# Involution weights laid out by frame row, and only the rows that are not zero written to DRAM

## The chip, the cores and the metric

The kernel runs on one core of one Trainium2 chip. The metric is the device time of one execution in microseconds. TensorE is PE in the profile, VectorE DVE, ScalarE ACT, GpSimd POOL, SyncE SP.

## What is computed

The input x is (32, 256, 32, 32). Two layers, each added to its input. The first is a group norm (32 groups of 8 channels) and a 3x3 convolution of 256 to 256 channels with values rounded to 16-bit floats. The second is a group norm and an involution: every pixel makes its own 7x7 kernel for each of 16 groups of 16 channels.

```python
# layer 1, xn = _gn(x)
y = relu(bn(einsum('oc,bchw->bohw', w1, xn)))              # 64 channels
w = einsum('oc,bchw->bohw', w2, y) + b2                    # 16 groups x 49 taps per pixel
w = w.reshape(b, G, K * K, H, W)
out = einsum('bgkhw,bgckhw->bgchw', w, patches)            # each output pixel: its 49 neighbours
x = x + out
```

## The kernel before, in words

The work goes image by image (32), and in each image by stages: 16 stages an image, of which every second has work of each kind. `front(b)` (L288 to L404) is a generator, run some 56 stages ahead of its image: group norm, the convolution (L336, 72 matmuls of 128x128 in 16-bit floats), second group norm into `xn`, the 64 channels `py` (L384), and the transposes `pt` (L399), copied to `pixels` (L403). `tc.manual_schedule()` (L549) keeps the order as the loop at L551 writes it, so every engine runs its instructions in this order; the framework adds the semaphores.

Multiplying each pixel by its own weights on TensorE is done by going through DRAM. A *frame* is a part of the image: 8 image rows (TR) by 16 columns (JC), in two halves of 4 rows (XR); each half of 64 partitions holds 4 rows x 16 columns as the contraction. An input pixel of a half adds to 10 rows (WIN = 4 + 7 - 1) by 22 columns of output around it. So for each input pixel a band row is wanted that holds, for each of 7 columns and 10 window rows, 16 groups: the weight where the output pixel is in reach of it, and zero elsewhere. The steps:

- `weights(b, r0)` (L406): 16 matmuls (each two instructions in the profile) make the weights `pw` of 4 image rows from `y_sb` and `w2_sb` (L414), for 32 columns in each of four column tiles.
- `evict` (L427) adds the bias on VectorE and writes them to the ring `w_sb` (L438). `w_sb` has 24 slots a pixel column, one for each image row. In this kernel a slot is [8 pairs of groups, 10 window rows, 2 groups of the pair], 160 floats of which three window rows are always zero; they are zeroed once (L207).
- `scatter(b, k, part)` (L468): seven DMAs a frame row, one per column tap, on SP's queue (L479). Each writes 32 columns x 8 rows of 160 floats (640 B) into the DRAM tensor `wd` [32 rows, 38 columns, 1128]. A pixel's record `WPIX` there is 7 x 160 floats and a padding of 8 floats that stays zero.
- `load_bands(b, k)` (L481): 16 DMAs a frame row bring, for pixel column j of both sides, 8 rows x 1128 floats (4512 B) to the partitions j, j+16, ... of a band tile. Successive rows are read `ROW - V` apart, so that each row lies shifted by one window row in its band. 14 of 16 go on POOL's queue, two on SP's (L491). There are three band tiles.
- `sums(b, m)` (L503): for both halves of groups h and both groups v of a pair, for both frame halves g and four column tiles t, one fp32 matmul (L517; two instructions in the profile). The moving operand `of` is taken from the band: 19 pixel columns (160 floats apart) by 10 window rows, for one group; at the image's upper and lower edge one of the two halves has 7 rows. It adds into `acc` in PSUM.
- `add_windows` (L525) adds `acc` to x on VectorE (L533); `store` writes x out.

The main loop puts, in each stage: the front's steps, `sums` of one frame, `add_windows` of the frame before, `weights` 18 stages ahead, `scatter`, the load of a later image (L590), `load_bands` three band tiles ahead. Before the loop, SP's queue gets, in order: image 0, the parameters, three zero fills of `wd` from a zeroed band (L200: the paddings of all 1216 records, and the side columns' taps that no scatter writes), and then image 1 and the following (L108). The profile's names: `wd<-w_sb` is the scatter, `band<-wd` the band load; L621 and L628 are the program's frame.

The two lines about which the rest turns:

```python
of = of.rearrange("p (j a r v) -> p j a r v", a=A, r=WIN, v=V)   # L514
of[:, :, a, f - top : l - top, v]                                  # L520, rows V = 2 floats apart
```

Of the kernel before, what the change touches and what calls it, by code (L numbers as in the profile page):

```python
# [9 lines left out]
F32 = mybir.dt.float32  # L10
# [3 lines left out]
P = 128  # L14
B, C, H, W = 32, 256, 32, 32
# [5 lines left out]
K1, PAD1 = 7, 3  # L21
TAPS = K1 * K1
CR = 64
G = 16
# [12 lines left out]
XR = 4  # L37
RG = 2
KP = P // RG
TR = RG * XR  # L40
SIDES = 2
JC = W // SIDES
K = H // TR
M = K * SIDES
WIN = XR + K1 - 1
WINC = JC + K1 - 1
WINI = JC + PAD1
# [4 lines left out]
V = 2  # L52
A = G // V
WB = G * WIN
PAD = V * (TR - XR)
WPIX = K1 * WB + PAD
SW = K1 * G
S = H + 2 * PAD1
T = 4
TW = P // T  # L60
PAIR = 3 * GC
PAIRS = G // 2
ROW = S * WPIX
WR = 4
NBAND = 3
SHARE = 8
NPIX = 6
RING = 24
# [6 lines left out]
def tile_quant_conv_then_involution(  # L75
# [16 lines left out]
    nc = tc.nc  # L92
    PSUM = bass.MemoryType.PSUM

    const = ctx.enter_context(tc.tile_pool(name="const", bufs=1))
# [47 lines left out]
    y_sb = [const.tile([P, N // 2], F32, name=f"y_{i}") for i in range(2)]  # L143
    bands = [const.tile([P, SIDES, WINC * WB + PAD], F32, name=f"band_{i}") for i in range(NBAND)]
    for t in bands[CH:]:
# [3 lines left out]
        nc.gpsimd.memset(t, 0.0)  # L149


    w_sb = const.tile([P, 2, RING, A, WIN, V], F32, name="w_sb")
    wd = dram.tile([H, S, WPIX], F32, name="wd")
    acc = [ps_acc.tile([P, RG, NT], F32, name=f"acc_{d}") for d in range(SIDES)]

# [9 lines left out]
    b2_sb = const.tile([P, 2, 2, SW], F32, name="b2_sb")  # L165
    for dj in range(K1):
        t, e = divmod(dj, 2)
# [19 lines left out]
    nc.vector.tensor_sub(bn_shift, bn[:, 1:2], bn_shift)  # L187


    for col, cols, at, n in (  # L190
        (0, S, K1 * WB, PAD),
        (PAD1, PAD1, 0, PAD1 * WB),
        (W, PAD1, (K1 - PAD1) * WB, PAD1 * WB),
    ):
        to = bass.AP(
            tensor=wd.tensor,
            offset=wd.offset + col * WPIX + at,
            ap=[[ROW, H], [WPIX, cols], [1, n]],
        )
        nc.sync.dma_start(to, bands[NBAND - 1][:H, 0, :n].unsqueeze(1).to_broadcast([H, cols, n]))  # L200

    def quantize_weights():

# [202 lines left out]
    def weights(b, r0):  # L406

        pws = [ps_w.tile([P, 2, 2, SW], F32, tag=f"pw{i}", name=f"pw{i}") for i in range(2)]
        for r in range(2):
            for t in range(T):  # L410
                for i in range(2):
                    half = slice(i * CR, (i + 1) * CR)
                    dj = slice(2 * t, min(2 * t + 2, K1))
                    nc.tensor.matmul(  # L414
                        pws[i][t * TW : (t + 1) * TW, : dj.stop - dj.start, r],
                        y_sb[b % 2][half, (r0 // 2 + r) * W : (r0 // 2 + r + 1) * W],
                        w2_sb[half, dj],
                        start=True,
                        stop=True,
                    )  # L420
        for i in range(2):
            for e in range(2):
                p = P if e == 0 else (K1 // 2) * TW
                for r, rows, d0, d1, at in ring_pieces(b, r0 + 2 * i):
                    evict(pws[i][:p, e, r : r + rows], e, r, rows, d0, d1, at)

    def evict(of, e, r, rows, d0, d1, at):  # L427

        p = of.shape[0]
        to = w_sb[:p, e]  # L430
        to = bass.AP(
            tensor=to.tensor,
            offset=to.offset + at * WB + V * (K1 - 1 - d0),
            ap=[to.ap[0], [V * WIN, rows * A], [WB - V, d1 - d0], [1, V]],
        )
        of = of.rearrange("p r (a d v) -> p (r a) d v", a=A, v=V)
        bias = b2_sb[:p, e, r : r + rows].rearrange("p r (a d v) -> p (r a) d v", a=A, v=V)
        nc.vector.tensor_tensor(to, of[:, :, d0:d1], bias[:, :, d0:d1], ALU.add)  # L438

    def ring_pieces(b, r0):  # L440
# [27 lines left out]
    def scatter(b, k, part):  # L468

        at = (b * H + k * TR) % RING  # L470
        for dj in range(part, K1, 2):
            t, e = divmod(dj, 2)
            to = bass.AP(
                tensor=wd.tensor,
                offset=wd.offset + k * TR * ROW + dj * WPIX + (K1 - 1 - dj) * WB,
                ap=[[WPIX, TW], [ROW, TR], [1, WB]],
            )
            rows = w_sb[t * TW : (t + 1) * TW, e, at : at + TR]
            nc.sync.dma_start(to, rows.rearrange("p s a r v -> p s (a r v)"))  # L479

    def load_bands(b, k):  # L481

        band = bands[(b * K + k) % NBAND]
        for i in range(JC):
            j = i // 2 + i % 2 * JC // 2
            src = bass.AP(
                tensor=wd.tensor,
                offset=wd.offset + k * TR * ROW + (j + PAD1) * WPIX,
                ap=[[ROW - V, TR], [JC * WPIX, SIDES], [1, WPIX]],
            )  # L490
            queue = nc.sync if i % SHARE == SHARE - 1 else nc.gpsimd  # L491
            queue.dma_start(band[j::JC, :, j * WB : j * WB + WPIX], src)  # L492

    def windows(b, m):


        k, d = divmod(m, SIDES)
        for g in range(RG):
            top = k * TR + g * XR - PAD1
            at = acc[d][:, g, : CH * WINI * WIN].rearrange("p (h j r) -> p h j r", h=CH, r=WIN)  # L500
            yield g, at, top, max(top, 0), min(top + WIN, H)

    def sums(b, m):  # L503

        k, d = divmod(m, SIDES)
        j0 = 0 if d else PAD1
        band = bands[(b * K + k) % NBAND][:, d]
        px = pixels[(b * K + k) % NPIX][:, d]
        for h in range(CH):
            for v in range(2):  # L510
                for g, at, top, f, l in windows(b, m):
                    p = slice(g * KP, (g + 1) * KP)
                    of = band[p, V * g * XR + j0 * WB : V * g * XR + (j0 + WINI) * WB]
                    of = of.rearrange("p (j a r v) -> p j a r v", a=A, r=WIN, v=V)  # L514
                    for t in range(T):
                        a = h * T + t
                        nc.tensor.matmul(  # L517
                            at[t * TW : (t + 1) * TW, h, :, f - top : l - top],
                            px[p, a, v * GC : v * GC + TW],
                            of[:, :, a, f - top : l - top, v],  # L520
                            start=(h, v) == (0, 0),
                            stop=(h, v) == (CH - 1, 1),
                        )
# [25 lines left out]
    with tc.manual_schedule():  # L549
        fronts = {}  # L550
        for n in range(FRONT, B * per + 2):  # L551
# [14 lines left out]
            if b is not None and i % 2 == 0:  # L566
                sums(b, i // 2)
# [14 lines left out]
            for part in range(2):  # L582
                b, i = due(n, -LEAD + 1 + part)
                if b is not None and i % 2 == 0:
                    for k in range(K):
                        if i // 2 == min((k + 1) * TR // WR, H // WR - 1):
                            scatter(b, k, part)
# [5 lines left out]
            if b is not None and i % 4 == 0:  # L593
                load_bands(b, i // 4)
# [37 lines left out]
```

## Time and profile before

| | |
|---|---|
| median of 3 runs | 1384.38 us (1379.81 to 1394.09) |
| the profiled execution's own time | 1388.26 us |
| its span, first to last instruction | 1386.5 us |
| PE busy, share of the span | 1265.7 us, 91% |
| DVE, ACT, POOL | 62%, 52%, 73% |
| granted PE clock, mean | 0.982 |
| DMA packets, bytes | 366568, 369.97 MB, mean 267 GB/s |
| `wd<-w_sb` | 896 DMAs of 160.0 KB |
| `band<-wd` | 1792 on POOL, 256 on SP, of 70.5 KB |
| waits: PE acc L517 on DMA band<-wd | 45.8 us in 21 waits |

How to read it. The span is one profiled execution; the few us around it make the device time. A busy share is the time in which at least one instruction of the engine runs; matmuls overlap, and the share of a line or form counts the union of its own. In a group's line, "x" is the number of instructions, then busy us and mean ns of one, then the idle time of the engine just before them and who ended it. The slices are 40 equal parts of the span, each digit the busy tenths. DMA share is the mean busy share of 16 engines. The chain of waits is followed back from the last instruction; "SPq" is SyncE's time to issue a DMA.

### The profile page before, as it was taken

How to read it: one execution, taken by the hardware profiler on the slowest of the kernel's cores; microseconds unless marked ns; L12 is line 12 of the kernel's file. 1: busy time of each engine (PE TensorE's matmuls, PEld its weight loads, DVE VectorE, ACT ScalarE, POOL GpSimd, SP SyncE). 2: the span in 40 equal slices, each digit the busy share in tenths (PEclk: the TensorE clock that was granted, in tenths of full speed). 3: DMA queues.
4: the chain of work that ended last, by engine and by line, in shares of the span. 5: the costliest groups of instructions: out<-in, count | busy, mean ns of one | idle time of the engine just before them, and what ended most of it. 6: DMA issues, size and time to landing. Idle time of an engine off the chain costs nothing.

```text
span 1386.5 us, 70020 instructions
## 1 busy us (share of the span) xinstructions
PE 1265.7 (91%) x29440; PEld 809.6 (58%) x29440; DVE 861.2 (62%) x3179; ACT 727.1 (52%) x1699; POOL 1010.0 (73%) x1818
## 2 busy tenths in 40 slices
PE   4799999999999999999999999999999998999763
PEld 2356666666665655566566666656666665656542
DVE  3366666666666666676676666657666675766542
ACT  4765555465646545665455565645556564553300
POOL 9067677687777777777768687777787767778785
PEclk9999999999999999999999999999999999999987
DMA  6089999999999999999999999999999999999995
GB/s 220 2 223 283 282 272 289 281 267 297 277 268 282 285 281 274 278 282 272 289 280 282 284 276 276 286 287 268 280 303 272 283 286 276 276 275 271 269 268 170
DMA packets 366568, 369.97 MB, mean 267 GB/s; under 512 B 78960, under 2 KB 308528, under 8 KB 366000
## 3 DMA queue, kind: packets, MB, share of 16 engines
q1 hardware_dynamic: 280240, 235.90, 57.6%
q0 software_dynamic: 86016, 129.60, 33.8%
q8 instruction: 234, 3.83, 1.2%
q14 instruction: 78, 0.64, 0.2%
HBM read 184.43 MB, written 180.76 MB: 263 GB/s over the span
## 4 chain that ended last, share of the span: by engine, by line
PE 58%; DMA 24%; POOL 5%; issue 4%; DVE 3%; ACT 3%; SPq 2%; POOLq 0%; DVEq 0%; ACTq 0%
PE pc L336 22%; PE acc L517 19%; DMA band<-wd 13%; PE pw L414 11%; DMA wd<-w_sb 9%; POOL band L492 5%; PE py L384 3%; PE pt L399 3%; DVE w_sb L438 2%; ACT junk L223 1%; SPq L479 1%; DMA w_sb<-in_w 1%; DVE x L533 0%; ACT xn L282 0%; DMA x<-in_x 0%
## 5 line engine op out<-in xcount | busy, mean ns | idle before, releaser
L492 POOL DMA_DIRECT2D band<-wd x1792 | 978.0, 548 | 363.0 <-DMA band<-wd 218.5
L438 DVE TENSOR_TENSOR w_sb<-pw,b_sb 128x16 f32<-128x16 f32 (+9 forms) x1920 | 373.7, 265 | 423.9 <-PE pw L414 403.5
L336 PE MATMUL pc<-xq,wq 128*128 128x496 f16 (+3 forms) x2304 | 535.8, 379 | 27.4 <-ACT xq L282 23.8
L517 PE MATMUL acc<-band,pixels 64*32 64x190 f32 (+1 forms) x16384 | 427.1, 330 | 68.5 <-DMA band<-wd 45.8
L336 PEld LDWEIGHTS <-wq 128*128 128x128 f16 x2304 | 206.8, 98 | 322.6 <-issue 110.1
L517 PEld LDWEIGHTS acc<-band,pixels 64*32 64x32 f32 x16384 | 301.7, 106 | 157.9 <-issue 86.1
L414 PE MATMUL pw<-w_sb,y 64*32 64x224 f32 (+1 forms) x8192 | 292.9, 332 | 17.0 <-issue 15.2
L533 DVE TENSOR_TENSOR x<-acc,x 128x380 f32<-128x380 f32 (+1 forms) x512 | 262.7, 513 | 32.8 <-PE acc L517 23.9
L414 PEld LDWEIGHTS pw<-w_sb,y 64*32 64x32 f32 x8192 | 187.7, 106 | 48.3 <-issue 31.1
L403 ACT COPY pixels<-pt 128x512 f32<-128x512 f32 x128 | 73.7, 576 | 237.5 <-PE pt L399 237.5
L223 ACT ACTIVATE junk<-x 128x512 f16<-128x512 f32 (+1 forms) x192 | 146.4, 763 | 20.1 <-DVE x L352 8.4
L223 ACT ACTIVATE junk<-x,mean 128x1024 f16<-128x1024 f32 x128 | 147.1, 1149 | 4.3
L254 ACT ACTIVATE s<-back,eps 128x2 f32<-128x2 f32 x64 | 18.9, 296 | 204.8 <-DVE back L239 204.7
L350 DVE TENSOR_SCALAR q<-pc 128x512 f16<-128x512 f32 x128 | 87.2, 682 | 19.3 <-PE pc L336 19.2
L282 ACT ACTIVATE xn<-x,off,rstd 128x512 f32<-128x512 f32 x128 | 96.2, 800 | 0.0
L352 DVE SCALAR_TENSOR_TENSOR x<-q,bias_sb,x 128x512 f32<-128x512 f16 x128 | 94.7, 740 | 0.3
L399 PEld LDWEIGHTS pt<-ident,xn 128*128 128x128 f32 x512 | 63.7, 142 | 25.9 <-issue 3.2
L399 PE MATMUL pt<-ident,xn 128*128 128x128 f32 x512 | 77.8, 275 | 0.1
L282 ACT ACTIVATE xq<-x,off,rstd 128x1024 f16<-128x1024 f32 x64 | 75.7, 1227 | 0.5 <-PE pc L336 0.5
L384 PEld LDWEIGHTS py<-xn,w_sb 128*64 128x64 f32 x2048 | 62.7, 138 | 16.6 <-issue 7.5
L244 ACT ACTIVATE mean<-back 128x2 f32<-128x2 f32 x64 | 12.7, 198 | 111.5 <-DVE back L239 111.4
L384 PE MATMUL py<-xn,w_sb 128*64 128x64 f32 x2048 | 67.6, 224 | 2.6 <-ACT xn L282 1.9
(40 smaller groups left out, 370.8 us busy)
## 6 DMA issues: line engine op xcount, KB each, us to landing
wd<-w_sb SPq DMA_DIRECT2D x896, 160.0 KB
band<-wd POOLq DMA_DIRECT2D x1792, 70.5 KB, 4.9
x<-in_x SPq DMA_DIRECT2D x64, 512.0 KB
out<-x SPq DMA_DIRECT2D x64, 512.0 KB
band<-wd SPq DMA_DIRECT2D x256, 70.5 KB
band<-in_w SPq DMA_DIRECT2D x2, 1152.0 KB
w_sb<-in_w SPq DMA_DIRECT2D x2, 196.0 KB
wd<-band SPq DMA_DIRECT2D x2, 180.0 KB
```

The costliest lines, as they stand in the source:

```text
L223: nc.scalar.activation(junk[:, n0:n1], src[:, h, n0:n1], func, bias=bias, accum_out=self.sums[:, i : i + 1])
L282: nc.scalar.activation(dst, src, AF.Identity, bias=self.off[:, one], scale=self.rstd[:, one])
L336: nc.tensor.matmul(pc.rearrange("p (r c) -> p r c", c=W)[:, r0 - nt * RT : r1 - nt * RT, c0:c1], wq[:, kh, k, mh * P : (mh + 1) * P], xq[: ...
L350: nc.vector.tensor_scalar(q, pc, F16_MAX, -F16_MAX, ALU.min, ALU.max)
L352: nc.vector.scalar_tensor_tensor(xt[:, mh, cols], q, bias_sb[:, mh : mh + 1], xt[:, mh, cols], ALU.add, ALU.add)
L384: nc.tensor.matmul(py[i * CR : (i + 1) * CR, cols], w1_sb[:, kh, :], px[:, r : r + 2], start=kh == 0, stop=kh == CH - 1,)
L399: nc.tensor.transpose(pt[:, i, h * P : (h + 1) * P], xn[:, h, (m + i) * P : (m + i + 1) * P], ident)
L414: nc.tensor.matmul(pws[i][t * TW : (t + 1) * TW, : dj.stop - dj.start, r], y_sb[b % 2][half, (r0 // 2 + r) * W : (r0 // 2 + r + 1) * W], w ...
L438: nc.vector.tensor_tensor(to, of[:, :, d0:d1], bias[:, :, d0:d1], ALU.add)
L492: queue.dma_start(band[j::JC, :, j * WB : j * WB + WPIX], src)
L517: nc.tensor.matmul(at[t * TW : (t + 1) * TW, h, :, f - top : l - top], px[p, a, v * GC : v * GC + TW], of[:, :, a, f - top : l - top, v], ...
L533: nc.vector.tensor_tensor(x_at, of, x_at, ALU.add)
```

## The change

A slot of `w_sb` becomes [7 rows, 16 groups], 112 floats, with no zeros. The scatter writes 112 floats (448 B) where it wrote 160. In `wd` a pixel's record keeps ten window rows for each of seven taps, now as [10 rows, 16 groups]; the padding becomes 16 x 4 = 64 floats, so a record has 1184 floats (4736 B). The three zero rows of each tap are no longer written by the scatter: `wd` is zeroed whole, once, at the place of the three small fills, by one DMA of 5.76 MB (32 x 38 x 4736 B) from a zeroed band on 32 partitions. Bands are loaded in records of 4736 B with rows `ROW - 16` apart. The moving operand of `sums` takes group a * 2 + v of each row: rows 16 floats apart. The columns of w2 and b2 are put in the new order on the host. Instructions, their number and order stay as they are, except that SP issues one fill in place of three.

```diff
-PAD = V * (TR - XR)
+SLOT = G * K1
+PAD = G * (TR - XR)
 WPIX = K1 * WB + PAD
...
-    w_sb = const.tile([P, 2, RING, A, WIN, V], F32, name="w_sb")
+    w_sb = const.tile([P, 2, RING, SLOT], F32, name="w_sb")
...
-    for col, cols, at, n in (
-        (0, S, K1 * WB, PAD),
-        (PAD1, PAD1, 0, PAD1 * WB),
-        (W, PAD1, (K1 - PAD1) * WB, PAD1 * WB),
-    ):
-        to = bass.AP(
-            tensor=wd.tensor,
-            offset=wd.offset + col * WPIX + at,
-            ap=[[ROW, H], [WPIX, cols], [1, n]],
-        )
-        nc.sync.dma_start(to, bands[NBAND - 1][:H, 0, :n].unsqueeze(1).to_broadcast([H, cols, n]))
+    zeros = bands[NBAND - 1][:H, 0, :WPIX].unsqueeze(1).to_broadcast([H, S, WPIX])
+    nc.sync.dma_start(wd, zeros)
...
-            offset=to.offset + at * WB + V * (K1 - 1 - d0),
-            ap=[to.ap[0], [V * WIN, rows * A], [WB - V, d1 - d0], [1, V]],
+            offset=to.offset + at * SLOT + G * (K1 - 1 - d0),
+            ap=[to.ap[0], [SLOT, rows], [SLOT - G, d1 - d0], [1, G]],
         )
-        of = of.rearrange("p r (a d v) -> p (r a) d v", a=A, v=V)
-        bias = b2_sb[:p, e, r : r + rows].rearrange("p r (a d v) -> p (r a) d v", a=A, v=V)
+        of = of.rearrange("p r (d g) -> p r d g", g=G)
+        bias = b2_sb[:p, e, r : r + rows].rearrange("p r (d g) -> p r d g", g=G)
...
-                ap=[[WPIX, TW], [ROW, TR], [1, WB]],
+                ap=[[WPIX, TW], [ROW, TR], [1, SLOT]],
             )
             rows = w_sb[t * TW : (t + 1) * TW, e, at : at + TR]
-            nc.sync.dma_start(to, rows.rearrange("p s a r v -> p s (a r v)"))
+            nc.sync.dma_start(to, rows)
...
-                ap=[[ROW - V, TR], [JC * WPIX, SIDES], [1, WPIX]],
+                ap=[[ROW - G, TR], [JC * WPIX, SIDES], [1, WPIX]],
...
-                    of = band[p, V * g * XR + j0 * WB : V * g * XR + (j0 + WINI) * WB]
-                    of = of.rearrange("p (j a r v) -> p j a r v", a=A, r=WIN, v=V)
+                    of = band[p, G * g * XR + j0 * WB : G * g * XR + (j0 + WINI) * WB]
+                    of = of.rearrange("p (j r g) -> p j r g", r=WIN, g=G)
...
-                            of[:, :, a, f - top : l - top, v],
+                            of[:, :, f - top : l - top, a * V + v],
```

The zero fill stands at L191 and L192 of the changed kernel, the scatter at L471, the band load at L484 and the matmul of `sums` at L509.

More of the change, by code (lines that the diff above doesn't have):

```diff
@@ L605 @@
     v = {name: np.asarray(a) for name, a in inputs.items()}
-    w2 = v["L1_conv_w2"].reshape(A, V, K1, K1, CR).transpose(4, 3, 0, 2, 1).reshape(CR, K1, K1 * G)
-    b2 = v["L1_conv_b2"].reshape(A, V, K1, K1).transpose(3, 0, 2, 1).reshape(K1, K1 * G)
+    w2 = v["L1_conv_w2"].reshape(A, V, K1, K1, CR).transpose(4, 3, 2, 0, 1).reshape(CR, K1, K1 * G)
+    b2 = v["L1_conv_b2"].reshape(A, V, K1, K1).transpose(3, 2, 0, 1).reshape(K1, K1 * G)
     laid_out = {
```

## The prediction

> **What bounds the kernel now.** I read the page's slices first, then stretches of the middle, then the groups by form, the waits and the start.
>
> ```profile
> PE   4799999999999999999999999999999998999763
> DMA  6089999999999999999999999999999999999995
> ...
> q1 hardware_dynamic: 280240, 235.90, 57.6%
> q0 software_dynamic: 86016, 129.60, 33.8%
> ```
>
> Two resources are full from the third slice to the third from the end: TensorE and the 16 DMA engines. The stretches say how full.
>
> ```profile
> core 0: us, PE busy (x) PEld busy (x) DVE busy (x) ACT busy (x) POOL busy (x), PEclk, DMA share, GB/s
> 600.00:643.00 43.00, 40.81 (x992) 26.89 (x976) 28.78 (x115) 23.76 (x57) 30.02 (x56) 0.96 1.00 288
> 700.00:743.00 43.00, 41.61 (x999) 26.81 (x979) 28.55 (x108) 22.69 (x54) 32.19 (x59) 1.00 0.99 284
> 1300.00:1343.00 43.00, 27.39 (x872) 20.35 (x880) 22.21 (x92) 3.26 (x6) 33.98 (x64) 0.92 0.92 267
> ```
>
> In the middle PE is idle for 2.19 and 1.39 us of 43 (mean 1.8) and DMA for nothing: both are bounds. The first `sums` matmul of image 0 starts at 93.9 us, of image 29 at 1277.9 (starts of L517 in the trace): 29 images in 1184.0 us, 40.8 each, PE idle about 1.7 of each (1.8 x 40.8/43) or 49 us in all. After 1278 no convolution is left, and there DMA (0.92) is ahead of PE. So relieving DMA alone can win at most the 49 us and a little at the end, while a microsecond added to PE's work per image is paid 29 times, less that same idle time.
>
> ```profile
> 703.41 1.56 PE L517 MATMUL acc<-band,pixels 64*32 64x190 f32 x64
> 704.65 1.07 PE L414 MATMUL pw<-w_sb,y 64*32 64x224 f32 x32
> 705.66 2.08 PE L336 MATMUL pc<-xq,wq 128*128 128x496 f16 x9
> ```
>
> From the timeline (start, length): one stage on PE. A `sums` call holds PE from 703.41 to 704.65, 1.24 us: 64 instructions, eight at once (two row halves, four column tiles), so eight turns of 155 ns.
>
> ```profile
> L517 PE MATMUL acc<-band,pixels 64*32 64x190 f32 x12288 | 424.4, 337 | 52.4 <-DMA band<-wd 32.1 <-issue 9.9 <-DMA wd<-w_sb 5.5
> L414 PE MATMUL pw<-w_sb,y 64*32 64x224 f32 x6144 | 290.7, 355 | 12.4 <-issue 11.0 <-DVE w_sb L438 1.0
> L517 PE MATMUL acc<-band,pixels 64*32 64x133 f32 x4096 | 184.4, 309 | 16.2 <-DMA band<-wd 13.7 <-issue 2.5
> L414 PE MATMUL pw<-w_sb,y 64*32 64x112 f32 x2048 | 180.2, 265 | 4.6 <-issue 4.1
> ```
>
> The groups by form (mean ns after the comma) price a column. L414 reads w2_sb without gaps: 112 columns more cost 355 - 265 = 90 ns, 0.80 ns a column. L517 reads rows 8 B apart, 19 pixel columns of 10 or 7 rows. Its 57 columns more should cost 46 ns; they cost 337 - 309 = 28. If instead rows are served in pairs and an odd row costs a whole pair, seven rows count as eight: 19 x 2 = 38 places x 0.80 = 30 ns. That fits. So the trace says that a row which shares its 16 B with no neighbour costs about two places.
>
> ```profile
> 22.28 0.67 SPq L200
> ...
> 23.00 0.73 SPq L200
> ...
> 23.77 0.43 SPq L200
> ...
> 24.24 0.44 SPq L108
> ...
> 24.72 5.63 DMA x<-in_x
> ```
>
> The chain at the start: the zero fills of L200, then the load of image 1 behind them on the same queue, then ScalarE, which waited 2.92 us for that load (its timeline at 29.19). This place has no slack.
>
> **The change part by part.** The instructions of each engine keep their kind, number and order; only SP has two DMAs less. Durations are those of the profiled execution: 1388.26 us, span 1386.5, and 3.9 above the median of 1384.38 that the forecast is to be held against.
>
> *The moving operand of L517.* `of` takes one group of 16 for each row: rows stand 64 B apart instead of 8. No two rows of a pixel share 16 B. From the odd row above, each of the 190 rows then costs two places: 190 x 0.80 = 152 ns more per turn. The half with 133 columns is always beside one with 190, which sets the turn. Eight turns, 1.22 us a call; eight calls, 9.8 us an image; 29 images, +284 us. PE has no room for it. Bounds: below, nothing, if the pairing is not what the odd row showed (the vector add L533 reads PSUM rows 40 B apart and takes 543 ns for 380 elements, as much per element as L352's 740 for 512, so strides are not dear everywhere). Above: the starts of successive matmuls on one tile in the trace have a median distance of 170 ns for 190 columns and 147 for 133, where 57 x 0.80 would leave 124; 23 ns over 19 odd rows is 1.2 ns each, so 230 ns a turn, 14.7 us an image, +427 us. I take 152, by the nearest row, the form that differs in nothing else.
>
> [...]
>
> *Scatter, L479.* 896 DMAs of 256 packets (229,376, as the trace's packet records have them), 640 B each, now 448 B. A 640 B packet takes 32 ns in the median, 36.0 in the mean. 448 B packets are in the trace, the loads of b2_sb: 25 ns in the median. The smallest writes to DRAM there, 32 B, take 7; on the line from 7 to 32, 448 B gives 24. I take 0.75 of the time: 9.0 ns x 229,376 / 16 engines = 129 us of engine time less. Bounds: 0.70 (bytes alone), and 55 ns a packet, what the slowest twentieth of the 640 B packets take (rival 3).
>
> [...]
>
> *Band loads, L492.* 2048 DMAs of 16 packets, 4512 B, now 4736: mean 242 ns x 5% x 32,768 / 16 = +25 us. Net DMA -104 us, 3.2 an image of some 40. What that buys: PE's idle time in the middle, 49 us, which is largely waiting for bands and buffers; a longer PE image hides the rest too. I take three quarters, -37; bounds 0 and -49. It can't be had twice, so once PE is the longer by 9.8, faster transfers bring nothing more.
>
> *The zero fill, L190.* One DMA of 1216 packets of 4736 B in place of three small ones, on SP's queue ahead of images 1 to 3. The old fill has 192 packets of 1920 B from the same 32 partitions, 148 ns each: at that rate 365 ns x 1216 / 16 = 27.7 us, less the old fills' 2.3: +25 us. Lower bound by the 640 B packets' rate, 20 B/ns: 18 - 2 = +16; by the 4512 B packets' 181 ns: 14.4 - 2.3 = +12. I take 25 because packet sources and moment are the same. Behind it: image 1's load, ScalarE's stream (in order, so image 0's second half too), the second convolution at 40.4. SP's two issues less save 1 us. Nothing later gives it back, since both bounds run at their rate from 94 us on.
>
> *Evictions, L438.* Runs of 16 instead of 2. 224 elements take 383 ns and 16 take 164, 1.05 ns an element already with runs of 2; nothing to win, and VectorE is 62% busy. *Memsets on POOL:* w_sb is 30% smaller (6.5 us, now 4.5), each band 1.6% larger; they end by 33 us, the first reader of w_sb comes at 62.
>
> *The last three images.* 35 to 37 us each, with DMA ahead; PE has some 12 us of room in each against +9.8. DMA is 3 us shorter. I take +2 in all.
>
> Sum: +284 - 37 + 25 + 2 = +274; 1388.3 + 274 = 1662 on the profiled execution, 1658 on the median.
>
> **The rivals.**
> 1. *Stride costs PE nothing (the other side, faster).* The turn stays at 155 ns, DMA falls under PE: -37 in the middle, -9 at the end (3 an image), +25 at the start: -21, 1363 on the median. With the fill at +12, 1350; with no idle time won back, up to 1395. For it: DMA at 1.00 and the waits for band<-wd; against it: the 133-column form. Each ns on a turn costs 64 x 29 = 1.86 us, so it decides as long as a turn grows by less than 11 ns.
> 2. *The single rows cost more than two places,* by the distances of starts: +427 - 49 + 25 + 9 (PE passes DMA in the last images as well) = +412, 1796. For it: the medians; against: the means by form. Between 1 and the forecast lies half a penalty, +142 - 37 + 25 = +130, 1514, if the four tiles, whose groups now lie 8 B apart, are served in part together.
> 3. *Short writes become dear and DMA the bound* without PE's penalty: packets at 55 instead of 36.0 ns, 19 x 229,376 / 16 = +272, bands +25, fill +25: 1706. For it: nothing in the rows; against: 32 B at 7 ns. Together with PE's penalty PE and DMA are about equal again, near 1720.
>
> **How the numbers follow.** Two places for each row 0.58 (with rival 3 on top or not): 1658, own range 1620 to 1720. Rival 2: 0.12. Half a penalty: 0.11. Rival 3 alone: 0.04. Rival 1: 0.15, of which 0.12 is under the bound of 1% (about what a measurement of this kernel can tell from no change) and 0.03 within it. Faster 0.12, same 0.03, slower 0.85. The range from 1500 to 1800 leaves out rival 1 and the edges of the half penalty.
>
> **What would show it.** Right: L517's 64x190 form about 150 ns longer and the 64x133 form about 90 (266 places for 152); `sums` calls about 2.4 us apart from the next L414 instead of 1.24; DMA share in the middle near 0.75 and PE without gaps; images 49 to 50 us apart; image 1's load landing near 55 us and the first L517 near 119; scatter packets at 24 to 25 ns. Wrong: L517's form unchanged (rival 1), or packets of 448 B at 50 ns and DMA still at 1.00 (rival 3). My sum fails first at the price of a single row, which the trace shows only one in seven at a time, never in a run.

## The result, and the profile after

The changed kernel takes 1633.46 us in the median (1633.11 to 1637.68), the kernel before 1387.32 beside it: a ratio of 1.1795, 95% interval 1.1752 to 1.1838, slower. The profiled execution took 1637.68 us with a span of 1635.9; its span is 249.4 us longer than that of before, where the working had +274.

The slices of the page of the kernel after, its queues and its memory traffic:

```profile
PE   4399999999999999999999999999999999999995
...
DMA  7458788877787877788877778877878877877796
...
q1 hardware_dynamic: 280016, 198.13, 44.0%
q0 software_dynamic: 86016, 136.02, 33.2%
...
HBM read 191.77 MB, written 142.07 MB: 204 GB/s over the span
```

PE is full and DMA no longer is: two bounds have become one. The start has changed too: the second and third slice of PE show 3 and 9 where 7 and 9 stood, in slices that are 18% longer.

The stretches of the kernel after (width, busy of each engine, PE clock, DMA share, GB/s):

```profile
600.00:643.00 43.00, 43.00 (x808) 27.46 (x807) 24.95 (x91) 21.98 (x52) 25.90 (x49) 1.00 0.76 198
700.00:743.00 43.00, 43.00 (x820) 27.85 (x809) 23.16 (x84) 21.17 (x47) 29.30 (x54) 1.00 0.79 197
1300.00:1343.00 43.00, 43.00 (x822) 27.26 (x827) 24.19 (x99) 21.51 (x51) 25.72 (x49) 1.00 0.77 201
```

PE is busy 43.00 of 43 us at clock 1.00, and it gets through 808 to 822 matmuls where it did 992 and 999. Nothing is awaited; the matmuls themselves are longer. DMA is at 0.76 to 0.79 (it was 1.00).

The timeline of PE of the kernel after, one stage (start, length):

```profile
727.53 3.05 PE L509 MATMUL acc<-band,pixels 64*32 64x190 f32 x64
730.12 1.21 PE L406 MATMUL pw<-w_sb,y 64*32 64x224 f32 x32
731.27 2.08 PE L328 MATMUL pc<-xq,wq 128*128 128x512 f16 x9
```

The `sums` call holds PE from 727.53 to 730.12, 2.59 us where it held it for 1.24; the convolution behind it is as long as before (2.08 us). The weights between them take 1.21 us here and took 1.07, but their matmuls are no longer, as the groups show. The groups by form of the kernel after (count, busy us, mean ns):

```profile
L509 PE MATMUL acc<-band,pixels 64*32 64x190 f32 x12288 | 745.6, 505 | 8.5 <-DMA band<-wd 8.5
L406 PE MATMUL pw<-w_sb,y 64*32 64x224 f32 x6144 | 348.6, 354 | 0.0
L509 PE MATMUL acc<-band,pixels 64*32 64x133 f32 x4096 | 281.5, 415 | 4.2 <-DMA band<-wd 3.1 <-issue 1.1
L406 PE MATMUL pw<-w_sb,y 64*32 64x112 f32 x2048 | 220.3, 265 | 0.0
```

The two forms of `sums` are 168 ns (337 to 505) and 106 ns (309 to 415) longer, where the prediction named about 150 and 90; the two forms of the weights are not longer at all (355 and 265 before). So it isn't the clock (1.00 here) and isn't PE as such: only the matmul whose operand's rows moved apart.

The start, from the chain of waits of the kernel after (start, length):

```profile
22.45 0.67 SPq L192
23.16 31.41 DMA x<-in_x
```

and from its ScalarE timeline (in brackets the idle time before and its releaser):

```profile
54.67 1.06 ACT L215 ACTIVATE junk<-x 128x1024 f16<-128x1024 f32 x1 [27.71 <-DMA x<-in_x]
```

The load of image 1 stood 5.63 us in the chain; now it stands 31.41, because the zero fill is ahead of it on its queue. ScalarE, which waited 2.92 us for it, waits 27.71. The granted PE clock is not behind the later start: it was 0.50 for longer (39.2 to 69.9 us, before 38.7 to 45.5), but from the end of that load to the first `sums` matmul it took 64.2 us, and 63.5 before.

By the starts of the `sums` matmuls in the trace the whole difference can be laid out:

| | before | after |
|---|---|---|
| first `sums` matmul | 93.9 us | 118.8 us |
| mean distance of images 0 to 29 | 40.83 us | 48.71 us |
| PE idle in these 29 images | 51.4 us | 0.0 us |
| PE's own time of an image (distance less idle) | 39.05 us | 48.71 us |
| from image 29 to PE's last instruction | 103.4 us | 99.0 us |

### The profile page after: what moved, and what is told of

It is laid out like the page before. It is cut to its first block, busy times and chain, and to the rows that moved or that the text cites. A ratio compares the mean times of both kernels' runs of the same rounds, so it can differ in the third digit from the quotient of the medians.

```text
span 1635.9 us, 70020 instructions
## 1 busy us (share of the span) xinstructions
PE 1563.9 (96%) x29440; PEld 997.0 (61%) x29440; DVE 862.5 (53%) x3179; ACT 730.8 (45%) x1699; POOL 1006.5 (62%) x1818
## 3 DMA queue, kind: packets, MB, share of 16 engines
HBM read 191.77 MB, written 142.07 MB: 204 GB/s over the span
## 4 chain that ended last, share of the span: by engine, by line
PE 91%; DMA 4%; ACT 2%; SPq 1%; DVE 1%; issue 1%; POOL 0%; POOLq 0%; ACTq 0%; DVEq 0%
PE acc L509 41%; PE pc L328 29%; PE pw L406 14%; PE py L376 4%; PE pt L391 3%; DMA x<-in_x 2%; ACT junk L215 1%; DMA band<-wd 1%; DMA w_sb<-in_w 1%; POOL band L484 0%; DMA wd<-w_sb 0%; SPq L180 0%; ACT xn L274 0%; DVE w_sb L430 0%; SPq L170 0%
## 5 line engine op out<-in xcount | busy, mean ns | idle before, releaser
L484 POOL DMA_DIRECT2D band<-wd x1792 | 977.4, 548 | 614.4 <-DMA wd<-w_sb 214.6
L509 PE MATMUL acc<-band,pixels 64*32 64x190 f32 (+1 forms) x16384 | 747.3, 482 | 12.6 <-DMA band<-wd 11.5
L509 PEld LDWEIGHTS acc<-band,pixels 64*32 64x32 f32 x16384 | 434.5, 119 | 200.9 <-issue 71.3
L406 PE MATMUL pw<-w_sb,y 64*32 64x224 f32 (+1 forms) x8192 | 348.7, 332 | 0.0
L406 PEld LDWEIGHTS pw<-w_sb,y 64*32 64x32 f32 x8192 | 250.9, 112 | 43.7 <-issue 8.2
```

The source lines that it names most:

```text
L406: nc.tensor.matmul(pws[i][t * TW : (t + 1) * TW, : dj.stop - dj.start, r], y_sb[b % 2][half, (r0 // 2 + r) * W : (r0 // 2 + r + 1) * W], w ...
L509: nc.tensor.matmul(at[t * TW : (t + 1) * TW, h, :, f - top : l - top], px[p, a, v * GC : v * GC + TW], of[:, :, f - top : l - top, a * V + v],
```

## The experiments

Two theories stood to be told apart. The one on record: a row that is alone in its 16 B (below: in its *line*) costs PE two *places*, a place being the time of one column, some 0.8 ns. Its rivals: the loss is DMA's (short runs, longer records, the fill); the loss is PE's but from the size of the step, from wide fetches or from four tiles whose groups now lie side by side. Where an edit makes PE read other numbers of the band, the text on record says so. Ratios are against runs of the kernel before on the same chip.

**Only the read, in the kernel before.**

```diff
-                    of = of.rearrange("p (j a r v) -> p j a r v", a=A, r=WIN, v=V)
+                    of = of.rearrange("p (j w) -> p j w", w=WB)
...
-                            of[:, :, a, f - top : l - top, v],
+                            of[:, :, a * V + v + 16 * (f - top) : a * V + v + 16 * (l - top - 1) + 1 : 16],
```

> The kernel before, with one edit: the moving operand of sums takes its rows 64 B apart from the same bands (it multiplies other numbers of the band; scatter, fills and bands are those of before). Theory (a row alone in its 16 B costs two places): the turn goes from 168 to about 320 ns, images come 48.7 us apart with PE never idle, so 93.9 + 29 x 48.7 + about 102 = 1608 us of span, ratio 1.16. Rival (the loss comes from the DMA side, the new runs, records and fill): the turn stays at 168 and the time at that of before, ratio 1.00.

Measured: 1607.56 us, ratio 1.1619 (1.1561 to 1.1677). Its groups by form and a stretch of the middle:

```profile
L517 PE MATMUL acc<-band,pixels 64*32 64x190 f32 x12288 | 743.4, 504 | 12.3 <-DMA band<-wd 10.9 <-DVE x L533 1.3
...
L517 PE MATMUL acc<-band,pixels 64*32 64x133 f32 x4096 | 282.2, 414 | 4.1 <-DMA band<-wd 4.1
```

```profile
600.00:643.00 43.00, 43.00 (x827) 26.17 (x814) 22.08 (x69) 19.97 (x48) 27.15 (x51) 1.00 0.84 236
```

504 and 414 ns, the numbers of the changed kernel (505 and 415), with scatter, fills and records as they were. Images come 48.65 us apart. One edit of the read is the whole loss per image; DMA's rival is out.

**All of the change but the read.**

```diff
-                    of = of.rearrange("p (j r g) -> p j r g", r=WIN, g=G)
+                    of = of.rearrange("p (j a r v) -> p j a r v", a=A, r=WIN, v=V)
...
-                            of[:, :, f - top : l - top, a * V + v],
+                            of[:, :, a, f - top : l - top, v],
```

> The changed kernel, with one edit: the moving operand takes its rows 8 B apart again (it multiplies other numbers of the band). Theory: the turn is back at 168 ns; the shorter scatter leaves DMA below PE, images come at PE's own 39.1 to 39.6 us, the fill still costs 25 us at the start: 118.8 + 29 x 39.4 + 99 = 1360 us, ratio 0.98 (0.97 to 0.995). Rival (short runs of 448 B are dear as soon as DMA is the bound): images at 41 us or more, 1405 us and up, ratio above 1.01.

Measured: 1371.81 us, ratio 0.991 (0.9866 to 0.9953).

```profile
L509 PE MATMUL acc<-band,pixels 64*32 64x190 f32 x12288 | 421.1, 337 | 34.0 <-DMA band<-wd 16.7 <-issue 9.0 <-DMA wd<-w_sb 5.0
```

The matmul is back at 337 ns, images come 39.49 us apart and the first `sums` stands at 120.0 us. Runs of 448 B are not dear here (images 40.83 us apart before, with 640 B). This is rival 1 of the prediction, as a kernel: 1363 was its forecast. PE keeps 0.9 us of idle time an image (25.6 in 29 images), where I had left it 0.4, but its own time is shorter too (38.61 us for 39.05). The span, 1370.0, is 10 us over the 1360 expected: 1 at the start, 3 in the images, and 6 at the end, where I had counted 99 us to PE's last instruction and the span ends 104.8 us after the start of image 29.

**Only the fill moved,** in the changed kernel.

```diff
-    nc.sync.dma_start(wd, zeros)
...
                 x_tiles[b] = load_x(b)
+                if b == 2:
+                    nc.sync.dma_start(wd, zeros)
```

> The changed kernel, with the zero fill issued behind the loads of images 1 and 2 instead of ahead of them. Theory (image 1's load waits behind the fill and nothing gives it back): the first sums at 94 us instead of 118.8, time 25 us less, 1609 us, ratio to the kernel before 1.16. Rival (the start is hidden by slack further on): within 5 us of the changed kernel, 1630 and up.

Measured: 1605.04 us, ratio 1.1581 (1.1533 to 1.1629; the changed kernel's is 1.1795), 28 us less than the changed kernel. First `sums` at 97.9 us. Its longest wait of ScalarE for a load of x (total, times, longest):

```profile
ACT junk L214 <- DMA x<-in_x: 2.4, 2, 2.2
```

The 27.71 us are gone. In the spans the run is 29.2 us shorter: 20.9 at the first `sums`, and 9.4 because the images come 48.39 us apart instead of 48.71. The second part is not the wait for image 1, and no run here tells why it came. Nor is the start sharp: in the runs without the large fill ahead of image 1, the first `sums` stands between 91.4 and 98.1 us.

**Both edits.**

> Both edits of the two runs before it: rows 8 B apart (other numbers of the band are multiplied) and the fill behind the loads of images 1 and 2. It leaves only the shorter scatter and the longer bands. Theory: 94 + 29 x 39.4 + 99 = 1336 us, ratio 0.963 (0.955 to 0.975): what leaving out the zeros is worth by itself, limited by PE. Rival (DMA was not a bound, the gain is hidden): ratio 1.00.

Measured: 1349.71 us (1337.16 to 1357.11), ratio 0.973 (0.9664 to 0.9795). Its stretches:

```profile
600.00:643.00 43.00, 42.60 (x1026) 27.43 (x1024) 29.23 (x110) 24.99 (x56) 35.73 (x66) 1.00 0.96 266
700.00:743.00 43.00, 43.00 (x1050) 27.91 (x1035) 29.77 (x108) 27.27 (x64) 35.22 (x65) 1.00 0.96 274
```

So leaving out the zeros, with the fill behind image 2, is worth some 33 us if PE's read is left alone: PE is then nearly full and DMA at 0.96. The profiled execution (span 1335.4) fell on the expectation by luck: a start 2.6 us earlier and images 3.2 us shorter in all made up for 5.7 us more at the end, and it is the fastest of four. The median is 1% above the expectation.

**What a row costs: 12, 16, 8 and 4 B apart,** in the kernel before, one run each. `STEP` is 3, 4, 2 or 1 floats; `AT` is `16 * a + v`, and 2 floats more in the third.

```diff
-                            of[:, :, a, f - top : l - top, v],
+                            of[:, :, AT + STEP * (f - top) : AT + STEP * (l - top - 1) + 1 : STEP],
```

> The kernel before with rows of the moving operand 12 B apart (other numbers of the band are multiplied). Counted by 16 B lines, the ten rows of a pixel column touch 7 lines with three shared (v = 0) or 8 with two shared (v = 1). Theory (a line costs two places whether one or two rows use it): 14 or 16 places instead of 10, mean 15, turns of 168 + 19 x 5 x 0.80 = 244 ns, images at 39.05 + 64 x 0.076 = 43.9 us, span about 1475. Rival (any step over 8 B costs the same): turns of 320 ns and 1610 us.

```profile
L517 PE MATMUL acc<-band,pixels 64*32 64x190 f32 x12288 | 591.8, 430 | 14.0 <-DMA band<-wd 12.0 <-DVE x L533 1.5 <-issue 0.5
```

Measured: 1471.64 us, span 1469.8 (expected 1475); images 43.81 us apart. Between 8 and 16 B the cost lies between, where the count of lines puts it.

> The kernel before with rows 16 B apart (other numbers of the band are multiplied). Theory: every row is alone in its 16 B, so the same 320 ns a turn and 48.7 us an image as at 64 B, span about 1608. Rival (wider fetches, or the four tiles' groups 8 B apart in one slot were the cost at 64 B; here the groups of the tiles lie 64 B apart): turns clearly below 300 ns.

```profile
L517 PE MATMUL acc<-band,pixels 64*32 64x190 f32 x12288 | 755.1, 516 | 10.6 <-DMA band<-wd 7.7 <-DMA wd<-w_sb 2.2 <-DVE w_sb L438 0.6
```

Measured: 1623.84 us, images 49.01 us apart. 16 B are as dear as 64 and a little more (span 1622.0, where 1608 was expected), and here the groups of the tiles lie 64 B apart: neither wide fetches nor the neighbourhood of the tiles explain the loss.

> The kernel before with rows 8 B apart, but starting 8 B further, in the middle of a 16 B line (other numbers of the band are multiplied). Ten rows then touch 6 lines instead of 5. Theory: 12 places for 10, turns of 168 + 38 x 0.80 = 198 ns, images at 39.05 + 64 x 0.030 = 41.0 us or a little more, span about 1395 to 1410. Rival (only the step counts, not where a line begins): turns of 168 ns, span within 1% of before.

```profile
L517 PE MATMUL acc<-band,pixels 64*32 64x190 f32 x12288 | 487.3, 373 | 22.9 <-DMA band<-wd 14.7 <-issue 4.1 <-DVE x L533 2.5
...
L517 PE MATMUL acc<-band,pixels 64*32 64x133 f32 x4096 | 190.1, 310 | 6.9 <-DMA band<-wd 4.3 <-issue 2.6
```

Measured: 1395.82 us (before on the same chip 1392.71), span 1394.0 (1395 to 1410 expected). The same step of 8 B, begun in the middle of a line: the form with ten rows, now on six lines, takes 373 ns instead of 337; the form with seven, on four lines as before, 310 instead of 309. The step isn't what counts, the line is. The kernel's time hardly shows it: images went from 40.83 to 41.15 us only, because PE's own time (40.67, it was 39.05) took up what it had been waiting.

> The kernel before with rows 4 B apart (other numbers of the band are multiplied). Ten rows touch 3 lines. Theory: a line costs two places at least and otherwise one place a row, so the turn stays near 168 ns and the time at that of before. Rival (a place is a line, so fewer lines are faster): turns of 110 to 130 ns.

```profile
L517 PE MATMUL acc<-band,pixels 64*32 64x190 f32 x12288 | 410.6, 332 | 45.9 <-DMA band<-wd 18.5 <-issue 16.4 <-DMA x<-in_x 6.0
...
L517 PE MATMUL acc<-band,pixels 64*32 64x133 f32 x4096 | 171.5, 290 | 19.5 <-DMA band<-wd 11.6 <-issue 7.8
```

Measured: 1379.57 us, 332 ns. Three lines for ten rows instead of five save 5 ns only: below one place a row it hardly goes here. The form with seven rows falls by more, from 309 to 290 ns: its odd row, which was alone in its line at 8 B, mostly shares a line at 4 B. This is the row of the trace from which the prediction took its price.

**A cheaper scatter that keeps the pairs.**

```diff
+RUN = WB - V * (WIN - K1)
...
-                ap=[[WPIX, TW], [ROW, TR], [1, WB]],
+                ap=[[WPIX, TW], [ROW, TR], [1, RUN]],
...
                 x_tiles[b] = load_x(b)
+                if b == 2:
+                    zero_fills()
```

> The kernel before, with two edits that keep its layout of row pairs: the scatter leaves out the six zeros at the end of each run (616 B instead of 640; ten small zero fills put zeros there once), and the fills are issued behind the loads of images 1 and 2. Theory (fewer scattered bytes are worth what PE still waits for DMA, and the start is worth what stands in front of image 1): packets at 31 instead of 32 ns, 0.45 us of DMA time an image, and 2 us at the start: 15 us less at most, ratio 0.99 (0.985 to 1.0). Rival (616 B is no multiple of 64 B and such packets cost more than the bytes they save): packets at 33 ns or more and ratio above 1.00.

Measured: 1386.73 us, ratio 1.0007 (0.998 to 1.0034). In the packet records 616 B take 32 ns in the median, as 640 B do, 35.8 in the mean for 36.0. Both theories missed: the bytes saved nothing and cost nothing. The start (first `sums` at 91.6 us, 2.3 earlier) is not seen in the median.

## Why the prediction was right, point by point

The forecast was 1658 us; 1633.46 was measured. Every term but the smallest, the last three images, went the way that was worked out. The sum was 24.6 us too long in the spans: some 4 from the operand, 14 from PE's idle time, 6 from the last images. The errors add up; none hides another.

- *The moving operand, +284.* PE's own time of an image rose from 39.05 to 48.71 us: 9.66 x 29 = +280. Turns, by the distance of starts on one tile, went from 170 to 323 ns, 153 more (152 was taken). The mean length of the form rose by more, 168 ns; the ends of matmuls are modelled, the starts are what PE's time goes by (64 x 153 ns is 9.8 us an image, 64 x 168 would be 10.8). The nearest row of the trace, seven rows counted as eight, carried a factor of two. The upper bound of 230 ns, from the medians of starts of the two forms, was too high. That the price came out within 1 ns is partly luck: at 16 B, with the same count of places, the turn rose by 169 ns (170 to 339). Four more runs bear out the price of two places a line at steps and starts that the prediction never had, with the means of the 64x190 form:

| rows apart | lines for ten rows | places worked out | form, ns | more than before, per place more |
|---|---|---|---|---|
| 8 B (before) | 5 | 190 | 337 | |
| 4 B | 3 | 190 | 332 | |
| 8 B, from mid-line | 6 | 228 | 373 | 36 / 38 = 0.95 ns |
| 12 B | 7 or 8 | 285 | 430 | 93 / 95 = 0.98 ns |
| 16 B | 10 | 380 | 516 | 179 / 190 = 0.94 ns |
| 64 B (after) | 10 | 380 | 505 | 168 / 190 = 0.88 ns |

 Taken together, the six rows say that for this operand a line costs two places whether one or two rows use it (an added place 0.88 to 0.98 ns in these means).

- *PE's idle time, -37.* All 51.4 us went. But the shorter scatter didn't win them: with the old scatter and the new read (the first experiment) the idle time is 0.0 as well, and the images are 48.65 us apart for 48.71. A longer PE image hid the transfers by itself. In the changed kernel leaving out the zeros is worth nothing that the times show (1605.04 with the fill moved, 1607.56 with the old scatter); only with the read left alone is it worth 33 us.
- *The zero fill, +25.* First `sums` at 118.8 instead of 93.9: +25.0. Moving the fill gave 28 us of the median back; by the spans 20.9 of 29.2 us are the start's. The price of 148 ns for 1920 B from the same 32 partitions was the right row: the fill's packets took 369 ns in the mean, where 365 was worked out.
- *The last three images, +2.* They took 4.4 us less. PE had room for its longer turns there, as I said, but I gave the shorter transfers nothing. The gain is theirs: from image 29 to PE's last instruction it took 99.0 to 100.1 us in the four kernels with runs of 448 B, and 101.7 to 104.5 in the seven others, whatever the read.
- *Scatter packets.* 24 to 25 ns were forecast for 448 B; the median is 25, the mean 27.7 (36.0 x 0.75 = 27.0). The shorter packet is not dearer here, though the bytes per ns fall a little (640 B in 36.0 ns is 17.8, 448 B in 27.7 is 16.2). What was read from HBM grew too; the page of before has

```profile
HBM read 184.43 MB, written 180.76 MB: 263 GB/s over the span
```

 and 191.77 after. The 7.34 MB more are the longer bands exactly: 32,768 records x 224 B.

- *Rivals.* Rival 1 (the stride is free) is refuted by the first experiment, rival 2 (more than two places) and the half penalty by the turns (153 ns more), rival 3 (short writes are dear) by the second experiment.

What stays open: the mean packet of the band's size went from 242 to 284 ns, the fill's 1216 among them (281 for the bands alone, 16% for 5% more bytes; 265 where PE's read is left alone); no run here tells why. It cost nothing here, since PE never waited. It is also open why rows 16 B apart cost more than rows 64 B apart (turns of 339 and 323 ns, forms of 516 and 505), since the count of lines is the same. A version that has the short scatter and the paired rows at once, with the reference's numbers, was not run. What stands in its way is not tried either: each band row is shifted by one window row, so the pairs of odd image rows would begin half a pair later than those of even ones.

## What to carry to other kernels

Before a layout is made shorter for DMA, count how many 16 B lines the rows of TensorE's moving operand touch (fp32 here; other types and the stationary operand were not varied): where every line served two elements the matmul's turn was 170 ns, and where each served one it was 323 to 339. Ask which of two full resources a change loads: here the time that the shorter scatter took off DMA was hidden once PE's images were the longer ones (48.71 us apart with it, 48.65 without). And see what is awaited behind a transfer that is put at the head of a queue once, at the start: the packets of the fill ran from 23.8 to 52.0 us, and the first `sums` matmul came 25.0 us later.

## What the runs showed that I had not expected

- Rows 4 B apart are read slightly faster than pairs: starts on one tile lie 161 ns apart instead of 170 (190 places; the form's mean is 332 ns instead of 337).
- Packets of 616 B take as long as those of 640 B (32 ns in the median), though 448 B take 25 and 32 B take 7: here packet time did not follow a small saving of bytes.
